# Cross attention in a Perceiver layer: another order at its first layer norm and in its last key block

## The chip, the core and the metric

The kernel runs on one core of a Trainium2 chip. Its time is the device time of one execution in microseconds (us). Five engines work side by side, each in the order of its own queue: TensorE (PE: matmuls into PSUM[...]), VectorE (DVE), ScalarE (ACT), GpSimd (POOL[...]) and SyncE (SP, which issues transfers). An instruction waits for the others by semaphores, and everything behind it in its queue waits with it.

## The reference

The layer is cross attention, self attention with relative positions and a gated attention block, each after a layer norm. The change touches the first:

```python
q = (query @ Wq + bq).reshape(Bq, Sq, H, DK)
k = (key @ Wk + bk).reshape(Bq, Sk, H, DK)
v = (value @ Wv + bv).reshape(Bq, Sk, H, DK)
scores = jnp.einsum('bqhd,bkhd->hbqk', q, k) / np.sqrt(DK)
attn = jax.nn.softmax(scores.reshape(H * Bq, Sq, Sk), axis=0).reshape(H, Bq, Sq, Sk)
out = jnp.einsum('hbqk,bkhd->bqhd', attn, v).reshape(Bq, Sq, H * DK)
return out @ Wo + bo
```

The query is layernorm(x), with 4 batches of 128 rows of 512; keys and values come from a context of 4 batches of 2048 rows. There are 16 heads of 32. The softmax runs over axis 0: for every pair of a query and a key, over the 64 combinations of head and batch. So a block of keys can be finished by itself: its maxima and sums run over heads and batches, not over other keys. All is float32.

## The kernel before

**Blocks.** The context is cut into 16 blocks n of 128 keys (NK = 16), and each block into 4 chunks c of 4 heads. For a chunk, `scores(n, c)` (line 277) writes 128 keys x 2048 numbers (4 heads x 4 batches x 128 queries) into four PSUM banks, two tiles of two banks. ScalarE copies them, half by half, to the tile `sg` (`scores_out`, line 298), and VectorE takes the running maximum `mx` of the same PSUM halves (`largest_of`, lines 305 and 307). After the fourth chunk, `largest_tail` (line 322) folds `mx` to one number per key and query. In the next block's turn each chunk is lowered by it (`shifted`, line 328, VectorE), put through the exponential (`exponentials_of`, line 337, ScalarE), and added up over heads and batches (`total`, lines 341 to 344, GpSimd; `total_tail` folds to `zs`). In the block after that, `inverse` (line 359) takes 1/z, `scaled` (line 328 again) multiplies each chunk by it, `attend` (line 372) multiplies with the values on TensorE into `pso`, and `accumulate` (line 385) adds `pso` to `acc`. So three blocks are in work at once: scores of n, exponentials of n-1, products of n-2.

**Projections.** `keys(n, c)` (line 220) and `values(n, b)` (line 227) are each four 128x512 matmuls into a bank of a pool of two (`bank`); ScalarE copies the bank out (lines 268 and 274), which frees it, and GpSimd adds the bias row of the values (line 275).

**The order** is written out by hand: each engine's queue holds its instructions in the order in which the Python code issues them. The banks of scores come from a pool of two tiles, so the next chunk's scores wait until both copies and both maxima of the last chunk have read theirs. Two engines don't read one PSUM tile at the same time here: the later in program order waits for the earlier. In blocks 0 and 1 a copy of one half and the maximum of the other stand in turn; from block 2 on both copies come first, then (`largest`, line 309) both maxima. `pso` has one bank.

**The start.** Keys of block 0; then `layernorm_T` (line 145) normalises x, and with `before` given it calls that after the normalisation, ahead of the four groups of transposes (`turned`, line 171, a pair of banks, ScalarE copies). Before is `values(0, 0)`. Then come four query projections (line 418), and in block 0's turn `values(0, c + 1)` ahead of each chunk's scores for c = 0, 1, 2; chunk 3 has `keys(1, 0)` there. `position_table` (line 111) is a generator that makes a table `pos` for the self attention in three steps: products on GpSimd; a matmul `pps`, a copy `prow` and two small transfers on SP's queue (through `pos_dram` into `posr`); a matmul `pflip` and the copy `pos`. The second step stands after scores (0,0), the third after those of (1,0).

**The end.** With l = 13, m = 14, n = 15: after the loop come the last attention product of block 13, block 15's `largest_tail`, its subtractions, exponentials and sums, the scalings of block 14, and the products. Half of chunk 2 and all of chunk 3 of block 15, and the sums that GpSimd made of the rest, are added up by TensorE: `sum_up` (line 508) multiplies by the identity into `ps_sum`. z is reduced from it (line 523). The output banks start from x1 (line 502) and collect `project_out` (line 529) as chunks of `acc` get ready; `layernorm_T(out_ps, ps_g, 1)` follows.

## Time and profile before

| | |
|---|---|
| median of 3 runs | 875.72 us (874.93 to 877.7) |
| the profiled execution | 875.97 us |
| its span in the profile | 874.1 us |
| TensorE busy | 830.6 us (95%) |
| VectorE, ScalarE, GpSimd busy | 628.2, 436.5, 430.6 us |
| first layer norm's transposes to the queries' first matmul | 22.8 to 26.3 us |
| last scores of block 15 | 599.7 to 600.8 us |
| last sum into `ps_sum` ends | 627.4 us |
| last output projection ends | 652.4 us |

In the profile's lines, "L227" is line 227 of the kernel before, the tiles follow as written <- read, then partitions x elements. A 128x512 float32 matmul shows as two records. The ends of matmuls are modelled, so records that follow each other overlap a little; from start to start a record of 512 columns takes 0.43 us at full clock. What stands in brackets is the idle time of the engine ahead of the group and what ended it.

### The profile page before, as it was taken

Reading aid. Unit: us, or ns where it says so; the run is one execution under the profiler, and the core shown is the slowest. Engines: PE = TensorE matmul, PEld = TensorE weight load, DVE = VectorE, ACT = ScalarE, POOL = GpSimd, SP = SyncE. Lnnn points to the kernel's source line nnn. Section 1 sums busy time; section 2 is a strip of 40 time slices with the busy share of each in tenths; the row PEclk is TensorE's granted clock in tenths of the full one; section 3 lists DMA queues with packets and bytes.
Section 4 is the critical chain, followed back from the end, with each engine's and each line's share of the span. In section 5 each row is a group of like instructions: output and inputs, shape, how many; then the busy total and the mean of one; then the engine's idle time right before and its main releaser. Section 6 shows DMA issues by size and latency. Waiting matters only on the chain. (4 is left out here: it accounts for less than half of the span.)

```text
span 874.1 us, 16373 instructions
## 1 busy us (share of the span) xinstructions
PE 830.6 (95%) x7061; PEld 447.9 (51%) x7061; DVE 628.2 (72%) x616; ACT 436.5 (50%) x721; POOL 430.6 (49%) x289
## 2 busy tenths in 40 slices
PE   9999999999999999999999999999898997779998
PEld 5454544554544545445445445544443466664564
DVE  2059788878888888888889888788861637556663
ACT  3357455564464554554554555644411736843671
POOL 1236666566656567575675665667500002512152
PEclk9999999999999999999999999999998998798999
DMA  8130010110101101010010101010100212001101
GB/s 300 50 124 2 1 49 1 49 49 1 50 1 49 49 2 49 1 49 13 37 49 1 49 1 49 1 36 15 49 28 21 96 50 98 1 2 51 49 1 49
DMA packets 10905, 35.53 MB, mean 41 GB/s; under 512 B 977, under 2 KB 1138, under 8 KB 8786
## 3 DMA queue, kind: packets, MB, share of 16 engines
q1 hardware_dynamic: 8402, 29.43, 9.7%
q10 hardware_dynamic: 1632, 3.15, 1.1%
q0 software_dynamic: 800, 1.93, 0.9%
q8 instruction: 55, 0.90, 0.4%
q14 instruction: 16, 0.13, 0.0%
HBM read 33.45 MB, written 1.05 MB: 39 GB/s over the span
## 5 line engine op out<-in xcount | busy, mean ns | idle before, releaser
L328 DVE TENSOR_TENSOR sg<-sg,stat 128x2048 f32<-128x2048 f32 x128 | 288.2, 2282 | 1.2
L337 ACT ACTIVATE sg<-sg 128x2048 f32<-128x2048 f32 x64 | 122.4, 1912 | 246.8 <-DVE sg L328 246.8
L227 PE MATMUL ps_v<-w_xattn_Wv,ct 128*128 128x512 f32 x512 | 231.5, 596 | 3.7 <-ACT v L274 3.7
L220 PE MATMUL ps_k<-ct,w_xattn_Wk 128*128 128x512 f32 x480 | 221.9, 605 | 0.8 <-ACT pos L142 0.8
L343 POOL TENSOR_TENSOR sm<-sm,sg 128x1024 f32<-128x1024 f32 x46 | 108.6, 2360 | 145.5 <-ACT sg L337 143.3
L307 DVE TENSOR_TENSOR mx<-mx,ps_s 128x1024 f32<-128x1024 f32 x96 | 117.2, 1221 | 78.1 <-ACT sg L298 65.9
L227 PEld LDWEIGHTS ps_v<-w_xattn_Wv,ct 128*128 128x128 f32 x512 | 95.8, 190 | 129.9 <-issue 113.5
L220 PEld LDWEIGHTS ps_k<-ct,w_xattn_Wk 128*128 128x128 f32 x480 | 86.2, 189 | 94.1 <-issue 86.1
L298 ACT COPY sg<-ps_s 128x1024 f32<-128x1024 f32 x128 | 124.2, 1020 | 7.2 <-DVE mx L305 3.5
L344 POOL TENSOR_TENSOR sm<-sm,sg 128x1024 f32<-128x1024 f32 x46 | 108.8, 2366 | 3.6
L275 POOL TENSOR_TENSOR v<-v,row_xattn_bv 128x512 f32<-128x512 f32 x64 | 81.6, 1276 | 40.0 <-ACT v L274 40.0
L734 POOL TENSOR_TENSOR lg<-lg,rs 128x512 f32<-128x512 f32 x16 | 16.3, 1041 | 120.9 <-issue 112.3
L285 PE MATMUL ps_s<-qT,kT 32*128 32x128 f32 x2048 | 75.7, 283 | 0.1
L372 PEld LDWEIGHTS pso<-sg,v 128*32 128x32 f32 x1920 | 48.8, 109 | 47.5 <-DVE mx L307 22.0
L285 PEld LDWEIGHTS ps_s<-qT,kT 32*128 32x128 f32 x2048 | 63.3, 186 | 18.0 <-issue 17.0
L372 PE MATMUL pso<-sg,v 128*32 128x128 f32 x1920 | 64.6, 276 | 3.7 <-DVE acc L385 2.1
L341 POOL TENSOR_TENSOR sm<-sg 128x1024 f32<-128x1024 f32 x16 | 37.9, 2366 | 45.3 <-ACT sg L337 45.2
L268 ACT ACTIVATE kT<-ps_k,bk 128x512 f32<-128x512 f32 x64 | 44.2, 694 | 10.4 <-PE ps_k L220 5.9
L274 ACT COPY v<-ps_v 128x512 f32<-128x512 f32 x64 | 36.4, 569 | 8.5 <-PE ps_v L227 8.4
L385 DVE TENSOR_TENSOR acc<-pso,acc 128x512 f32<-128x512 f32 x54 | 37.0, 684 | 3.9 <-PE pso L372 3.9
L305 DVE TENSOR_TENSOR mx<-sg,ps_s 128x1024 f32<-128x1024 f32 x16 | 19.5, 1220 | 27.3 <-ACT sg L298 27.3
L964 POOL TENSOR_TENSOR e<-e,rs 128x512 f32<-128x512 f32 x16 | 16.3, 1041 | 41.8 <-DVE rs L963 41.8
(208 smaller groups left out, 817.0 us busy)
## 6 DMA issues: line engine op xcount, KB each, us to landing
ct<-in_ctxT SPq DMA_DIRECT2D x15, 1024.0 KB, 4.9
ev_win<-in_tabv SPq DMA_DIRECT2D x1, 2048.0 KB, 7.1
w_xattn_Wk<-in_xattn_Wk ACTq DMA_DIRECT2D x4, 256.0 KB, 8.0
ct<-in_ctxT SPq DMA_DIRECT2D x4, 256.0 KB, 6.7
x<-in_x SPq DMA_DIRECT2D x4, 256.0 KB, 8.2
w_xattn_Wv<-in_xattn_Wv ACTq DMA_DIRECT2D x1, 1024.0 KB
w_xattn_Wq<-in_xattn_Wq SPq DMA_DIRECT2D x1, 1024.0 KB, 10.3
w_xattn_Wo<-in_xattn_Wo ACTq DMA_DIRECT2D x1, 1024.0 KB, 5.4
```

The lines of the kernel that those rows point to most:

```text
L220: nc.tensor.matmul(ps, lhsT=w[:, k, c * P : (c + 1) * P], rhs=src[:, k, :], start=(k == 0), stop=(k == C - 1))
L227: nc.tensor.matmul(ps, lhsT=src[:, k, b * T : (b + 1) * T], rhs=w[:, k, :], start=(k == 0), stop=(k == C - 1))
L268: nc.scalar.activation(kT[n, c], ps, AF.Identity, bias=bk[:, c : c + 1])
L275: nc.gpsimd.tensor_tensor(v[n, b], v[n, b], bv_row, ALU.add)
L285: nc.tensor.matmul(ps[i][:, cols], lhsT=kT[n, c][rows, cols], rhs=qT[rows, c, cols], start=True, stop=True)
L298: nc.scalar.copy(sg[n, c][:, k * HALF : (k + 1) * HALF], pss[n, c][k])
L307: nc.vector.tensor_tensor(mxs[n], mxs[n], pss[n, c][k], ALU.max)
L328: nc.vector.tensor_tensor(g, g, stat[:, row, :].unsqueeze(1).to_broadcast([P, NH * B, T]), op)
L337: nc.scalar.activation(sg[n, c], sg[n, c], AF.Exp, scale=SCALE)
L343: eng.tensor_tensor(t, t, g[:, 0:HALF], ALU.add)
L344: eng.tensor_tensor(t, t, g[:, HALF:], ALU.add)
L372: nc.tensor.matmul(ps[i * HD : (i + 1) * HD, b * T : (b + 1) * T], lhsT=v[n, b][:, h * HD : (h + 1) * HD], rhs=sg[n, c][:, f * T : (f + 1) ...
```

## The change

- **Layer norm 0.** `layernorm_T` takes a second callback, `after`, called behind the transposes. `values` is split into the matmuls (`values_into`) and copy plus bias (`values_out`). Values (0,0) go to the bank of `pso`, so the transposes have the pair of banks to themselves, and are copied out after the copies of the transposes. Values (0,1) follow there, ahead of the queries.
- **Block 0.** Values (0,2) and (0,3) stand at c = 0 and 1, where (0,1) and (0,2) stood; at c = 2 there is no projection. `pflip` and `pos` stand after scores (0,2).
- **The last chunk's maxima (15,3)** are taken in turn with the copies.
- **The end.** `scaled(13, 3)` and `accumulate(13, 2)` move behind the four subtractions of block 15, and `attend(13, 3)` behind the sums. Each projection `values(15, 1..3)` stands behind an exponential, from that of chunk 0 on. All of chunk 2 is summed by TensorE and none of it by GpSimd. `attend(14, 2)` moves behind `attend(15, 0)`. Values (15, 1..3) are held in the pool `tmp`, since block 13's are needed longer.

```diff
             before()
             for b in range(B):
                 turned(b)
+            after()
...
-        def values(n, b):
-            v[n, b] = vp.tile([P, D], F32, tag="v", name=f"v{n}_{b}")
-            ps = bank(f"v{n}_{b}")
+        def values(n, b, ps=None):
+            values_out(n, b, values_into(n, b, bank(f"v{n}_{b}") if ps is None else ps))
+
+        def values_into(n, b, ps):
             project(ps, wv, cts[n], b)
+            return ps
+
+        def values_out(n, b, ps):
+            if n == NK - 1 and b:
+                v[n, b] = tmp.tile([P, D], F32, tag="xn", name=f"v{n}_{b}")
+            else:
+                v[n, b] = vp.tile([P, D], F32, tag="v", name=f"v{n}_{b}")
             nc.scalar.copy(v[n, b], ps)
             nc.gpsimd.tensor_tensor(v[n, b], v[n, b], bv_row, ALU.add)
...
-            if n < 2:
+            if n < 2 or (n, c) == (NK - 1, C - 1):
                 for k in (1, 0):
                     scores_out(n, c, k)
                     largest_of(n, c, 1 - k)
...
-            if n >= 2:
+            if n >= 2 and (n, c) != (NK - 1, C - 1):
                 largest_of(n, c, 0)
                 largest_of(n, c, 1)
...
-        xT = layernorm_T([x1[:, b, :] for b in range(B)], ps_g, 0, before=lambda: values(0, 0))
+        ps = ps_o.tile([P, B * T], F32, tag="pso", name="ps_v0_0")
+        xT = layernorm_T(
+            [x1[:, b, :] for b in range(B)],
+            ps_g,
+            0,
+            before=lambda: values_into(0, 0, ps),
+            after=lambda: (values_out(0, 0, ps), values(0, 1)),
+        )
...
-                elif n == 0 and c + 1 < C:
-                    values(0, c + 1)
+                elif n == 0 and c + 2 < C:
+                    values(0, c + 2)
...
                 if n == 0 and c == C - 2:
+                    next(position)
...
                     exponentials_of(0, c)
                     total(0, c)
-                    if c == 0:
-                        next(position)
...
                         inverse(n - 2)
+                    if (n, c) == (NK - 1, C - 1):
+                        break
                     scaled(n - 2, c)
...
-        m, n = NK - 2, NK - 1
-        attend(*done)
+        l, m, n = NK - 3, NK - 2, NK - 1
         largest_tail(n)
-        values(n, 1)
-        shifted(n, 0)
-        exponentials_of(n, 0)
-        total(n, 0)
+        for c in range(C):
+            shifted(n, c)
+            exponentials_of(n, c)
+            if c < 2:
+                total(n, c)
+            if c + 1 < C:
+                values(n, c + 1)
+        scaled(l, C - 1)
         accumulate(*done)
-        values(n, 2)
-        shifted(n, 1)
-        exponentials_of(n, 1)
-        total(n, 1)
-        shifted(n, 2)
-        exponentials_of(n, 2)
-        values(n, 3)
-        half_total(n, 2)
-        shifted(n, 3)
-        exponentials_of(n, 3)
         inverse(m)
         scaled(m, 0)
-        scaled(m, 1)
...
-        sum_up(sg[n, 2][:, HALF:], True, False)
+        sum_up(sg[n, 2], True, False)
         sum_up(sg[n, 3], False, False)
         sum_up(sms[n], False, True)
-        attend(m, 0)
-        attend(m, 1, bank("m1"))
+        attend(l, C - 1)
+        attend(m, 0, bank("m0"))
+        scaled(m, 1)
         scaled(m, 2)
...
         inverse(n)
-        attend(m, 2, bank("m2"))
+        attend(m, 1, bank("m1"))
...
         scaled(n, 0)
+        accumulate(l, C - 1)
         attend(n, 0, pso[m, 0], True)
         accumulate(n, 0)
         scaled(n, 1)
+        attend(m, 2)
         project_out(0, range(B - 1))
```

More of the change, by code (lines that the diff above doesn't have):

```diff
@@ L143, in position_table, with layernorm_T @@
         yield
-    def layernorm_T(src, pool, n, before=None):
+    def layernorm_T(src, pool, n, before=None, after=None):
         st = small.tile([P, B, 6], F32, tag="st", name=f"st{n}")
```

## The prediction

> **What bounds the kernel now.** I read the page first, then the timeline of the two stretches that the diff touches (0 to 112 and 570 to 662 us), then busy time and clock in 2 us windows. Page, part 1:

> ```profile
> PE 830.6 (95%) x7061; PEld 447.9 (51%) x7061; DVE 628.2 (72%) x616; ACT 436.5 (50%) x721; POOL 430.6 (49%) x289
> ```

> TensorE is busy 95%, and 99.4 to 99.6 of each 100 us from 200 to 600: in the sixteen-block loop it is the bound. So what the change does ahead of block 2 is carried to the end at its full size; what it does at the other end counts by the chain there. Timeline of the start (start, length, engine, line; in brackets the idle time before and its releaser):

> ```profile
> 26.28 14.00 PE L220 MATMUL ps_q<-xT,w_xattn_Wq 128*128 128x512 f32 x32 [0.68 <-ACT xT L215]
> ...
> 50.00 3.70 PE L227 MATMUL ps_v<-w_xattn_Wv,ct 128*128 128x512 f32 x8
> 50.00 4.06 SPq L431 DMA_DIRECT2D ct<-in_ctxT  x2
> 50.10 2.55 DVE L307 TENSOR_TENSOR mx<-mx,ps_s 128x1024 f32<-128x1024 f32 x2 [2.95 <-PE ps_s L285]
> 50.16 1.01 ACT L298 COPY sg<-ps_s 128x1024 f32<-128x1024 f32 x1 [0.57 <-PE ps_s L285]
> ...
> 51.36 1.01 ACT L298 COPY sg<-ps_s 128x1024 f32<-128x1024 f32 x1 [0.18 <-DVE mx L307]
> ...
> 53.63 1.17 PE L285 MATMUL ps_s<-qT,kT 32*128 32x128 f32 x32
> ```

> Scores (0,1) start at 48.90; their four banks come free at 52.37 (second copy) and 52.65 (second maximum), 3.5 and 3.75 later. A `values` projection (50.00 to 53.6) lies over that, so scores (0,2) wait for nothing. Next, who releases the first attention product:

> ```profile
> 92.24 0.96 DVE L359 RECIPROCAL stat<-z 128x128 f32<-128x128 f32 x1 [5.16 <-POOL z L319]
> ```
> ```profile
> 95.58 1.08 PE L372 MATMUL pso<-sg,v 128*32 128x128 f32 x32 [0.21 <-DVE sg L328]
> ```

> TensorE meets a chain that hangs on block 0's last scores, not on TensorE's own pace: maxima, subtraction, copies, second exponential, six POOL additions and three folds from 74.90, reciprocal, scaling. At the end, TensorE and VectorE:

> ```profile
> 602.92 1.08 PE L372 MATMUL pso<-sg,v 128*32 128x128 f32 x32 [2.08 <-DVE acc L385]
> ...
> 625.41 1.99 PE L508 MATMUL ps_sum<-sm,ident 128*128 128x512 f32 x4 [1.10 <-POOL sm L352]
> ```
> ```profile
> 604.41 2.54 DVE L307 TENSOR_TENSOR mx<-mx,ps_s 128x1024 f32<-128x1024 f32 x2 [1.54 <-ACT sg L298]
> ```

> The last sums end at 627.40, and the reduction of z follows at 627.43; VectorE was done with (14,2) at 626.2. So 1.2 us is all that can be won there. Windows after the block loop (PE, PEld, DVE, ACT, POOL, then clock):

> ```profile
> 654.00:656.00 2.00, 1.31 (x8) 0.83 (x8) 1.06 (x4) 1.92 (x5) 0.00 (x0) 1.00 0.96 355
> 656.00:658.00 2.00, 1.58 (x8) 1.34 (x8) 1.56 (x3) 2.00 (x5) 0.00 (x0) 0.64 0.37 142
> 658.00:660.00 2.00, 1.17 (x3) 0.50 (x2) 0.82 (x2) 0.34 (x1) 0.00 (x0) 0.50 0.00 0
> ```

> The clock halves at 656.6 (0.64 is 28% at full, the rest at half) and is back at 663.4. Ahead of the drop TensorE was busy some 1.5 of 3.4 us.

> [...] the second copy (51.36) starts as the first maximum on its half ends.[...] 43% busy sufficed at 656.6, while 629.3 to 632.7 (windows of 3.4 counted back from there), with 58% busy, did not drop. My estimate of the limit is half a window.

> **Start, part by part.** (a) Layer norm: (0,0)'s copy goes behind the four xT copies, and its bank out of their pair. The second group of transposes no longer waits (0.24); groups three and four wait for a copy each, the fourth group at 24.65 (24.95 before). Values (0,1) start at 25.3 when the third copy is done; queries at 28.8, +2.5 against 26.28. The moved projection is 3.5, so 1.0 is gained. On POOL two bias additions stand ahead of five DMA issues, which so start near 30.7, not 24.9; the tabk0 product ends near 37.2, needed at 47.2: nothing. (b) Scores (0,0) at 46.1, (0,1) at 51.4 under the cover of values (0,3). (c) For (0,2) no projection is left. Scores (0,1) issue until 52.5; banks are free at 51.4 + 3.5 = 54.9 and 55.1. TensorE is idle 2.4 us, and (0,2) end issuing at 56.15 against 54.73: +1.4. (d) pflip now follows. It reads posr: prow 2.5 later, posr issued at 52.1, landing 4.5 later (DMA issues view) at 56.6; SP's ct load behind it is needed 16 us after it lands. Wait 0.45, pflip 0.33: keys (1,0), queued behind it, at 57.0 against 54.73, +2.25; scores (0,3) and VectorE's maxima wait for these. The pos copy leaves ScalarE's stretch between exponentials (0,0) and (0,1): -0.15. Old pflip and the 0.81 wait for pos at 70.60 lay beside the chain: their removal brings TensorE to the first attention product at +1.2 only, where it waits, since the chain from scores (0,3) through POOL to z is at 2.25 - 0.15. **Start: +2.1**; from +1.2 (POOL spans are rough; were its chain loose, TensorE alone counts) to +2.8 (posr a little later).

> (e) The clock. From 52.5 to 57.0 TensorE works 1.2 us on scores and 0.33 on pflip. With 2.4 to 2.85 idle, a 3.4 us window falls under half in about three of four phases. Half clock for one window then slows scores and keys (1,0), on the path, by 1.0 to 1.6. Over the phases I take 0.8; bounds 0 and 1.6.

> **End.** (f) Scores (15,3) issue until 600.77. First maximum 600.87 to 602.1; ScalarE passes exponential (14,3), a value copy and the half copy, 603.46; second maximum to 604.7 (606.95 before). Tail 1.97: subtraction (15,0) ends at 609.0, the others every 2.23 us until 615.7. Exponential (15,0) is done at 611.0. (g) TensorE: values (15,1) and (15,2) until 607.75. Values (15,3) needs the bank of (15,1), whose copy now stands behind exponential (15,0): 611.5. Behind it are queued x1, the sums and so z. That is 3.7 us idle in place of the old 2.08, 0.39, 0.30 and 1.10 with their drains. Then 8 records for values, 8 for x1, 20 for sums at 0.4286 (24 took 10.3): 15.4, done at 627.2 with the last drain of 0.27, against 627.40. POOL is ready at 619.5; leaving out the half total frees it, but four more sum records (1.7) are TensorE's. VectorE reaches (14,2) at 626.2 as before: scaling (13,3) and its accumulation are moved, not removed. (h) z is 0.15 earlier; attention (14,2), 1.0, fills the 0.81 wait after (15,0). Attention (15,1) starts at 636.2 both times (636.24 before). **End: -0.05**; from -0.8 to +0.4.

> (i) Its clock. A gap of 3.7 holds more than half a window at any phase. Half clock for a window, less what falls into the gap, costs 0.7 to 1.7 on values, x1 and sums, all ahead of z. I take 1.1; bounds 0 and 1.7. Other edits (tmp buffers for v, loop order, sg held longer: nine of ten buffers) cost nothing: no queue waits for them.

> **Sum.** 2.1 + 0.8 - 0.05 + 1.1 = +3.9: span 874.1 to 878.0. The profiled execution took 875.97, so 1.9 lies around the span; it is 0.25 above the median of 875.72. Median: 875.7 + 3.9 = 879.6.

> **Rivals.** (1) The clock holds in both gaps. For: a 2.08 gap at 600.8 left it at 1.00. Against: 656.6. Time 875.7 + 2.05 = 877.8, not slower by what can be told; it decides if a window needs to be nearly empty. (2) The bubble before (0,2) is hidden, since VectorE or POOL has slack that the trace doesn't show, and the layer norm's 1.0 is balanced by a small loss: 875 to 876. Against: the chain to z is continuous from 74.90. (3) Both ends pay: -1.0 at the layer norm and -1.2 at z, some 873.3, up to 0.8 less with the filled wait. It decides at a bubble under 1.0, that is banks free within 2.1 of the start of scores (0,1); the trace has 3.5, two turns of some 1.2 after 1.2 of scores.

> **How the numbers follow.** Forecast (a clock drop at one end at least, 878.4 to 882) 0.62; rival 1, 0.22; rival 2, 0.09; rival 3, 0.07. A measurement of this kernel tells 0.3%, 2.6 us, from no change. Slower 0.62, same 0.31, faster 0.07. Case range 878.4 to 882; the range of 875.5 to 882 takes in rival 1 and part of rival 2 and leaves some 0.18 outside.

> **What would show it.** Right: queries start near 28.8; a TensorE gap of 2.4 ahead of scores (0,2) released by ACT sg or DVE mx; pflip waits for posr; the first attention product near 97.7 or later; a gap of 3.7 ahead of values (15,3) released by ACT v; z reduced near 627.3 plus the start's shift; clock 0.5 after either gap. Wrong: no gap at (0,2), or z more than 1 us earlier than the shift allows.

## The result and the profile after

The changed kernel takes 881.56 us (median of 5, 878.66 to 884.54) against 875.72 us (874.93 to 877.7): ratio 1.0058, 95% interval 1.0031 to 1.0084. It is slower, by less than 1%. Timed again with 21 executions, it took 881.24 against 877.20, ratio 1.0034 (1.0025 to 1.0044). The forecast was 879.6, which is +3.9; the two measurements are +5.8 and +4.0 by their medians, +5.1 and +3.0 by their ratios.

The page's first part of the changed kernel:

```profile
PE 833.7 (95%) x7065; PEld 449.5 (51%) x7065; DVE 628.0 (71%) x616; ACT 435.6 (49%) x721; POOL 427.6 (49%) x288
```

TensorE is busy 3.1 us more. Four more sum records are 1.7 of it; the rest is put down to records at half clock. To see where the added time went, both profiled executions (875.97 and 882.15 us) are cut at the same instructions:

| stretch (us) | before | after | difference |
|---|---|---|---|
| span's start to first matmul of values (0,0) | 19.34 | 20.38 | +1.04 |
| from there to the first attention product ("start") | 76.24 | 80.36 | +4.12 |
| to scores (15,3) | 504.09 | 503.96 | -0.13 |
| to the reduction of z ("end") | 27.76 | 29.32 | +1.56 |
| to the last group of output projections ("tail") | 20.35 | 20.35 | 0.00 |
| to the span's end | 226.32 | 226.03 | -0.29 |
| span | 874.1 | 880.4 | +6.3 |

The first row is no effect of the change: its work begins after it, and over the nine profiled executions of the experiments it lies anywhere from 19.41 to 20.52. The two ends hold the rest. TensorE's timeline at the start (columns as in the prediction):

```profile
26.42 3.70 PE L228 MATMUL ps_v<-w_xattn_Wv,ct 128*128 128x512 f32 x8 [0.19 <-ACT xT L216]
29.95 13.90 PE L221 MATMUL ps_q<-xT,w_xattn_Wq 128*128 128x512 f32 x32
...
52.47 1.17 PE L294 MATMUL ps_s<-qT,kT 32*128 32x128 f32 x32
55.99 1.44 PE L294 MATMUL ps_s<-qT,kT 32*128 32x128 f32 x32 [2.35 <-ACT sg L307]
58.29 0.79 PE L141 MATMUL ps_pflip<-flip,posr 128*128 128x128 f32 x2 [0.86 <-DMA posr<-pos_dram]
58.88 4.93 PE L221 MATMUL ps_k<-ct,w_xattn_Wk 128*128 128x512 f32 x8
...
100.74 1.08 PE L381 MATMUL pso<-sg,v 128*32 128x128 f32 x32 [0.88 <-DVE sg L337]
```

Less the 1.04, values (0,1) start at 25.4, the queries at 28.9, scores (0,1) at 51.4; then come 2.35 idle for the banks, released by ScalarE's copy (54.93 to 55.94; it had itself waited 0.18 for VectorE's maximum of the same half), and 0.86 for `posr`. Keys (1,0), behind pflip in the queue, start at 58.88 and take 4.93 where eight records take 3.6 at full clock. VectorE shows what lies ahead of the attention product: the same wait for z from GpSimd as before, only later.

```profile
97.40 0.96 DVE L368 RECIPROCAL stat<-z 128x128 f32<-128x128 f32 x1 [5.25 <-POOL z L328]
```

The end, TensorE, then VectorE, then ScalarE:

```profile
605.80 7.13 PE L228 MATMUL ps_v<-w_xattn_Wv,ct 128*128 128x512 f32 x16
616.57 5.40 PE L228 MATMUL ps_v<-w_xattn_Wv,ct 128*128 128x512 f32 x8 [3.63 <-ACT v L283]
621.80 3.60 PE L511 MATMUL ps_out<-x,ident 128*128 128x512 f32 x8
625.24 7.03 PE L517 MATMUL ps_sum<-sg,ident 128*128 128x512 f32 x16
632.10 1.88 PE L517 MATMUL ps_sum<-sm,ident 128*128 128x512 f32 x4
```
```profile
605.91 1.22 DVE L316 TENSOR_TENSOR mx<-mx,ps_s 128x1024 f32<-128x1024 f32 x1 [0.82 <-PE ps_s L294]
608.51 1.22 DVE L316 TENSOR_TENSOR mx<-mx,ps_s 128x1024 f32<-128x1024 f32 x1 [1.38 <-ACT sg L307]
...
634.02 0.69 DVE L533 TENSOR_REDUCE z<-ps_sum 128x128 f32<-128x512 f32 x1 [3.01 <-PE ps_sum L517]
```
```profile
614.13 1.91 ACT L346 ACTIVATE sg<-sg 128x2048 f32<-128x2048 f32 x1 [4.74 <-DVE sg L337]
615.95 0.57 ACT L283 COPY v<-ps_v 128x512 f32<-128x512 f32 x1
```

The maxima do end earlier, and the copy that frees the bank for values (15,3) does stand behind exponential (15,0): TensorE idles 3.63. VectorE has 3.01 to spare before z, so TensorE sets z. Its eight value records took 5.40 where 3.70 is usual: these 1.7 us are the clock's.

Busy time by engine in windows of 3.41 us, the length of the shortest period of half clock in this profile (PE, PEld, DVE, ACT, POOL, then granted clock, DMA share and GB/s); the edges are counted from where half clock begins:

```profile
54.70:58.12 3.42, 1.44 (x32) 1.25 (x32) 2.24 (x3) 1.70 (x3) 3.42 (x3) 1.00 0.67 215
58.12:61.53 3.41, 3.24 (x6) 1.69 (x7) 1.61 (x2) 1.55 (x3) 1.29 (x2) 0.50 0.90 377
...
614.51:617.92 3.41, 1.35 (x3) 0.68 (x4) 3.41 (x2) 3.41 (x3) 2.92 (x3) 1.00 0.00 0
617.92:621.33 3.41, 3.41 (x5) 1.35 (x4) 3.41 (x3) 2.69 (x3) 3.41 (x3) 0.50 0.00 0
```

After a window with TensorE busy for 1.44 (42%) and after one with 1.35 (40%), the next whole window runs at 0.50.

### The profile page after: what moved, and what is told of

It reads as the page before. It is cut to its first block, busy times and chain, and to the rows that moved or that the text cites. A ratio compares the mean times of both kernels' runs of the same rounds, so it can differ in the third digit from the quotient of the medians.

```text
span 880.4 us, 16375 instructions
## 1 busy us (share of the span) xinstructions
PE 833.7 (95%) x7065; PEld 449.5 (51%) x7065; DVE 628.0 (71%) x616; ACT 435.6 (49%) x721; POOL 427.6 (49%) x288
## 3 DMA queue, kind: packets, MB, share of 16 engines
HBM read 33.45 MB, written 1.05 MB: 39 GB/s over the span
## 4 chain that ended last, share of the span: by engine, by line
DVE 35%; PE 32%; ACT 21%; issue 11%; POOL 1%; DMA 1%; ACTq 0%; DVEq 0%; POOLq 0%
DVE sg L337 14%; DVE mx L316 12%; ACT sg L307 10%; ACT sg L346 4%; ACT v L283 3%; DVE stat L331 3%; PE s_k L221 3%; PE s_v L228 3%; PE ps_v L228 3%; PE ps_k L221 2%; DVE mx L314 2%; PE s_q L221 2%; PE s_y L1063 2%; PE ps_k L409 2%; PE s_q L228 2%
## 5 line engine op out<-in xcount | busy, mean ns | idle before, releaser
L352 POOL TENSOR_TENSOR sm<-sm,sg 128x1024 f32<-128x1024 f32 x46 | 108.5, 2359 | 145.5 <-ACT sg L346 143.4
L307 ACT COPY sg<-ps_s 128x1024 f32<-128x1024 f32 x128 | 124.1, 1020 | 8.1 <-DVE mx L314 3.5
```

Of the source, the lines that this page charges most:

```text
L307: nc.scalar.copy(sg[n, c][:, k * HALF : (k + 1) * HALF], pss[n, c][k])
L352: eng.tensor_tensor(t, t, g[:, 0:HALF], ALU.add)
```

## The experiments

Theory: the start is slower by a wait that the moved projection uncovers, with half clock on top; the end has no more than the clock's part. Rivals: the end alone makes the loss; the wait costs nothing and only the clock does; or the position table's step is what delays the keys. All kernels compute the whole reference; one has two extra matmuls, named below. Times are given as ratios to the kernel before on the same chip, with 95% intervals. The stretches come from one profiled execution each. The last column is the granted clock of a whole execution, as the mean over all executions of the kernel (their number in brackets), then the same for the kernel before on that chip. One more window of half clock lowers it by 0.002 (half of 3.41 us in some 876):

| kernel | start | end | tail | ratio | mean clock; before |
|---|---|---|---|---|---|
| before | 76.24 | 27.76 | 20.35 | 1 | |
| changed, first profile | 80.36 | 29.32 | 20.35 | 1.0058 (1.0031 to 1.0084) | 0.9786 (5) |
| e1, start undone | 76.22 | 30.38 | 20.34 | 0.9993 (0.9978 to 1.0008) | 0.9817 (14); 0.9798 (43) |
| e2, end undone | 79.63 | 27.74 | 22.04 | 1.0037 (1.0024 to 1.0050) | 0.9782 (6); 0.9798 (43) |
| e3, cover back | 76.27 | 29.34 | 20.34 | 0.9995 (0.9983 to 1.0007) | 0.9811 (14); 0.9798 (43) |
| e4, x1 first | 79.41 | 26.24 | 20.33 | 1.0009 (1.0000 to 1.0018) | 0.9817 (21); 0.9798 (43) |
| e0, changed again | 79.86 | 27.62 | 20.35 | 1.0034 (1.0025 to 1.0044) | 0.9791 (21); 0.9800 (34) |
| e5, filler | 78.16 | 29.18 | 20.35 | 1.0023 (1.0012 to 1.0035) | 0.9811 (14); 0.9800 (34) |
| e6, flip back | 79.46 | 29.32 | 20.35 | 1.0030 (1.0018 to 1.0043) | 0.9804 (16); 0.9803 (19) |
| e8, both mended | 75.62 | 26.23 | 21.99 | 0.9949 (0.9936 to 0.9961) | 0.9832 (5); 0.9800 (34) |
| e7, GpSimd scales | 75.63 | 24.88 | 20.02 | 0.9932 (0.9919 to 0.9945) | 0.9836 (5); 0.9800 (34) |

The diffs are against the changed kernel, unless said otherwise.

### e1: the start undone

```diff
-            before=lambda: values_into(0, 0, ps),
-            after=lambda: (values_out(0, 0, ps), values(0, 1)),
-        )
+        xT = layernorm_T([x1[:, b, :] for b in range(B)], ps_g, 0, before=lambda: values(0, 0), after=lambda: None)
...
-                elif n == 0 and c + 2 < C:
-                    values(0, c + 2)
+                elif n == 0 and c + 1 < C:
+                    values(0, c + 1)
...
                 if n == 0 and c == C - 2:
-                    next(position)
...
+                    if c == 0:
+                        next(position)
```

> The change's end with the start of the kernel before. Theory (lost cover in block 0 and half clock after it, +4.1 at the start; copies behind exponentials and half clock, +1.6 at the end): 875.7 + 1.6 = 877.3 us, first attention product where it was (about 95.6), gap of 3.6 us ahead of values (15,3) and half clock after it still there. Rival (the end alone costs the time, and the start's lateness is a later first matmul): 880 to 881 us.

The start is 76.22, as before. The end in the profiled execution is 30.38, with two windows of half clock, more than in the changed kernel. Yet by its times (median 876.13 of 14, where 877.3 was expected) the kernel equals the one before. The profiled execution took 879.47, the slowest of the 14: it overstates the end. The mean clock of all 14 is 0.9817, above the 0.9798 of the kernel before: over whole executions, the new end with the old start brings no more half clock than the old kernel had.

### e2: the end undone

The kernel before with only the start's edits: the callbacks of the layer norm, `c + 2`, and pflip after scores (0,2). The end is line for line the old one.

> The change's start with the end of the kernel before. Theory: 875.7 + 4.1 = 879.8 us; the 2.4 us gap ahead of scores (0,2) stays, the first attention product about 4 us late against the first matmul, and the last sums end about 28 us after the last scores, as before. Rival (the end alone costs): 875.7 to 876.5 us.

Start +3.39, and 0.37% by time, 3.2 us of 877.6 (2.0 by the medians of 6 and 43 executions). So the start makes the significant part of the loss. In this profiled execution half clock also fell on the tail, which is the old code here. TensorE's timeline of e2:

```profile
637.75 4.54 PE L541 MATMUL ps_out<-w_xattn_Wo,acc 128*128 128x512 f32 x6 [0.81 <-DVE acc L391]
```

Six records took 4.54 where 2.8 is usual: half clock strikes in the old end too, in some executions. Another window of it, from 607.2 on, slowed the last projections of block 15 (24 records in 11.30 us, 10.57 before), and yet the end is 27.74: the old end's waits of 0.39, 0.30 and 1.10 ahead of the sums shrank to one of 0.73 and took it up. The execution of before which the prediction was made from had half clock in neither place.

### e3: the cover back

One condition: values (0,2) and (0,3) stand ahead of scores (0,1) and (0,2) again, as in the kernel before, with the rest of the change kept. Ahead of scores (0,0) nothing stands now.

```diff
-                elif n == 0 and c + 2 < C:
-                    values(0, c + 2)
+                elif n == 0 and 0 < c < C - 1:
+                    values(0, c + 1)
```

> The changed kernel with values (0,2) ahead of scores (0,1) and values (0,3) ahead of scores (0,2), and nothing ahead of scores (0,0). Theory (the cover of scores (0,2) is what is lost): no 2.4 us gap ahead of scores (0,2), no half clock there; scores (0,0) wait 0.9 us for the last query copy, which the layer norm's filling pays; start at about -0.2 to +0.2, time 877.3 us as with the start undone. Rival (the layer norm's new order itself is late, or pflip's wait is what costs): 880 to 881.5 us.

TensorE's timeline of e3:

```profile
49.70 3.70 PE L228 MATMUL ps_v<-w_xattn_Wv,ct 128*128 128x512 f32 x8
53.33 1.17 PE L294 MATMUL ps_s<-qT,kT 32*128 32x128 f32 x32
```

The projection covers the turns of copies and maxima, scores (0,2) wait for nothing, the clock holds, and the start is 76.27. The wait of 0.9 that was expected ahead of scores (0,0) isn't there: they follow the queries at 43.05. With the new end in place the ratio is 0.9995, so this one condition undoes the whole of the measured loss.

### e4: x1 first

The four identity matmuls that put x1 into the output banks wait for nothing that block 15 makes. They move into the gap.

```diff
+            if c == 2:
+                out_ps, _ = banks("out")
+                for b in range(B):
+                    nc.tensor.matmul(out_ps[b], lhsT=ident, rhs=x1[:, b, :], start=True, stop=False)
             if c + 1 < C:
                 values(n, c + 1)
...
-        out_ps, _ = banks("out")
-        for b in range(B):
-            nc.tensor.matmul(out_ps[b], lhsT=ident, rhs=x1[:, b, :], start=True, stop=False)
```

> The changed kernel with the eight matmuls of x1 moved ahead of values (15,3), where TensorE waits 3.6 us. Theory (gap and half clock are on the path to z): gap under 0.4 us, clock at 1.00 there, sums end before VectorE is through with scaling (14,2), z about 2.6 us earlier against the last scores; 881.6 - 2.6 = 879.0 us. Rival (z isn't on the path, or VectorE's tail sets the end): less than 0.5 us gained, 881 us or more.

TensorE's timeline of e4:

```profile
611.16 3.60 PE L505 MATMUL ps_out<-x,ident 128*128 128x512 f32 x8
614.96 3.70 PE L228 MATMUL ps_v<-w_xattn_Wv,ct 128*128 128x512 f32 x8 [0.20 <-ACT v L283]
```

and VectorE's:

```profile
622.72 6.68 DVE L337 TENSOR_TENSOR sg<-sg,stat 128x2048 f32<-128x2048 f32 x3
629.32 0.68 DVE L534 TENSOR_REDUCE z<-ps_sum 128x128 f32<-128x512 f32 x1
```

The gap of 3.63 became 0.20, and the end is 26.24, 1.5 under that of before. z now follows VectorE's third scaling without a wait: VectorE sets it. By time the kernel gains about 0.25% on the changed one (878.14 on one chip, 881.24 on another, each against its own before).

### e0: the changed kernel again

> The changed kernel once more, beside the others on one chip. Theory: some 5 us above the kernel before; from the first values to the first attention product 79.4 to 80.5 us (76.2 before), from the last scores to the reduction of z 29 to 30.5 us (27.8 before), from there to the last output projections 20.35 us as before. Rival (the two chips differ more than the two kernels): less than 2.6 us above.

The same gap, without the clock's part, first in the timeline of TensorE and then by windows:

```profile
615.56 3.70 PE L228 MATMUL ps_v<-w_xattn_Wv,ct 128*128 128x512 f32 x8 [3.63 <-ACT v L283]
```
```profile
610.28:613.69 3.41, 1.65 (x4) 0.38 (x2) 3.38 (x3) 0.57 (x1) 3.33 (x4) 1.00 0.00 0
613.69:617.10 3.41, 1.54 (x4) 0.83 (x5) 3.41 (x2) 3.41 (x3) 2.97 (x3) 1.00 0.00 0
617.10:620.51 3.41, 3.41 (x10) 1.50 (x9) 3.41 (x3) 3.41 (x5) 3.41 (x3) 1.00 0.04 7
```

The edge fell almost at the middle of the gap. Both windows keep 48% and 45% of work, and the clock stayed at 1.00. The end is then 27.62, 0.14 under that of before, where 29 to 30.5 was expected; the time, +4.0 by medians, is under the 5 expected too. The start, 79.86, is as expected: half clock came again there (43% busy in the window ahead of it). This profiled execution is the fastest of the 21 (878.15), as e1's was the slowest of its own.

### e5: a filler in the start's gap

Two more 128x512 matmuls stand ahead of scores (0,2); nobody reads what they write.

```diff
+                if (n, c) == (0, C - 2):
+                    ps = ps_o.tile([P, B * T], F32, tag="pso", name="filler")
+                    for k in range(2):
+                        nc.tensor.matmul(ps, lhsT=cts[0][:, k, 0:P], rhs=wv[:, k, :], start=True, stop=True)
                 scores(n, c)
```

> The changed kernel with two matmuls of 128x512 more, whose result nobody reads, in the 2.4 us gap ahead of scores (0,2). Theory (the lost cover is 2.3 to 2.7 us by itself, half clock another 0.9 to 1.4): clock stays at 1.00, keys (1,0) take 3.7 us again, first values to first attention product 78.5 to 79.1 us, about 1 us below the changed kernel. Rival (the wait alone, or posr, sets the lateness, whatever the clock): as the changed kernel, or up to 1.7 us above it by the added work.

TensorE's timeline of e5:

```profile
53.13 1.98 PE L471 MATMUL filler<-w_xattn_Wv,ct 128*128 128x512 f32 x4
55.55 1.44 PE L294 MATMUL ps_s<-qT,kT 32*128 32x128 f32 x32 [0.44 <-ACT sg L307]
57.19 0.49 PE L141 MATMUL ps_pflip<-flip,posr 128*128 128x128 f32 x2 [0.20 <-DMA posr<-pos_dram]
57.52 3.60 PE L221 MATMUL ps_k<-ct,w_xattn_Wk 128*128 128x512 f32 x8
```

Scores (0,2) start no earlier, but keys (1,0) take 3.60: full clock. What remains, +1.92, is the wait's own price (2.3 to 2.7 was expected); the half clock is the other 1.7 of e0's +3.62. It isn't this one execution only: the mean clock of all 14 is 0.9811, and 0.9791 for e0 on the same chip, which is one window of half clock less in the mean. By time it is 0.11% under e0, with intervals that overlap: the stretches separate the two, the times hardly do.

### e6: pflip back in block 1

```diff
                 if n == 0 and c == C - 2:
-                    next(position)
...
+                    if c == 0:
+                        next(position)
```

> The changed kernel with one edit: the third step of the position table (the matmul pflip and the copy pos) stands in block 1 again, after scores (1,0), as before. The gap ahead of scores (0,2) stays. Theory of step (d): keys (1,0) wait no more for posr (0 to 0.86 in the executions so far) nor for pflip (0.33), so the stretch from the first matmul of values (0,0) to the first attention product shrinks from 79.9 to 80.4 to some 79.0, with the half clock in it, or to 77.6 if the clock holds; the gap ahead of scores (0,2) reads 2.35 again. Rival: keys (1,0) or scores (0,3) wait for something else at the same time (the banks of scores (0,2), the copies of keys), and the stretch stays within 0.3 of 79.9. Time by the theory 0.5 to 1.0 us under the changed kernel, by the rival none; both within what the rounds can tell, so the stretch decides.

TensorE's timeline of e6:

```profile
55.38 1.44 PE L294 MATMUL ps_s<-qT,kT 32*128 32x128 f32 x32 [2.35 <-ACT sg L307]
56.76 5.36 PE L221 MATMUL ps_k<-ct,w_xattn_Wk 128*128 128x512 f32 x8
```

The start is 79.46, between theory (79.0) and rival (79.6 at least), so neither number was met. Keys (1,0) follow the scores at once, so nothing else waits there and the rival's mechanism is absent. The window of half clock (56.72 to 60.13) falls wholly on work and costs its full 1.7; the theory's number had 1.4 for it. That leaves +1.5 for the wait. By time it can't be told from e0.

### e8 and e7: both ends mended, and GpSimd scales

e8 joins e3, e4 and e6. e7 adds this to it, with 1/z of block 14 copied to a tile of its own (`inv`) by ScalarE:

```diff
+        def scaled_pool(n, c):
+            g = sg[n, c].rearrange("p (f q) -> p f q", q=T)
+            nc.gpsimd.tensor_tensor(g, g, inv.unsqueeze(1).to_broadcast([P, NH * B, T]), ALU.mult)
...
         scaled(m, 1)
-        scaled(m, 2)
+        scaled_pool(m, 2)
+        scaled_pool(m, 3)
...
-        scaled(m, 3)
```

> The changed kernel with values (0,2) and (0,3) at chunks 1 and 2, pflip back in block 1, and x1 ahead of values (15,3). Theory: start -0.75 us against before (scores (0,2) covered, pflip off the chain), end -1.5 us; 2.2 us below the kernel before. Rival (VectorE's and ScalarE's chains set both ends anyway): within 0.5 us of the kernel before.

> As e8, and the scalings of (14,2) and (14,3) go to GpSimd, which is idle then, from a copy of 1/z in SBUF. Theory (z waits for VectorE's scaling once TensorE's gap is filled): z 1.4 us earlier than in e8, tail up to 0.6 us shorter; 3.5 to 4 us below the kernel before. Rival (GpSimd's two scalings, 4.7 us each, come late, or slow VectorE beside them): a TensorE wait ahead of attention (14,2) of 1 us or more, no gain over e8.

e8: start -0.62, end -1.53, and a window of half clock in the tail (+1.6); 873.58 us against 877.20, ratio 0.9949. So the change's ideas are worth something at both ends once the gaps are closed: 0.6 is the layer norm's 1.0 less small losses (scores (0,0) start 23.40 after the first values, 24.30 before; 0.62 of this 0.90 is left at scores (0,2)), and it shows once pflip, with its wait of 0.54 for `posr`, is off the path, which e3 (76.27) had not done. e7's VectorE and GpSimd timelines:

```profile
624.86 0.69 DVE L543 TENSOR_REDUCE z<-ps_sum 128x128 f32<-128x512 f32 x1 [0.44 <-PE ps_sum L526]
```
```profile
622.29 9.08 POOL L517 TENSOR_TENSOR sg<-sg,inv 128x2048 f32<-128x2048 f32 x2
```

With one scaling taken from ahead of z, z waits 0.44 for TensorE's sums again, and the end is 24.88, 2.9 under that of before. e7 takes 872.17 us (871.26 to 873.01) against 877.20: ratio 0.9932, faster than both kernels. No wait ahead of attention (14,2) shows, so the rival of late scalings is absent.

Both kernels gained more than was expected (2.2 and 3.5 to 4), and more than start, end and tail add up to: 0.5 for e8 in its profile, 3.8 for e7, where the medians fell by 3.6 and 5.0. Their mean clock is higher than that of before by one and a half to two windows of half clock, over five executions each. Why they meet fewer was not tested, so the gain beyond the stretches is not shown to be the edits' own.

## Why the prediction came out as it did

The direction, the places and the order of causes were right. The clock was mis-sized at both ends: too low at the start, and at the end counted for the new kernel alone.

**(a), (b), layer norm.** Predicted +2.5 for the queries against the first values; measured +2.63 (9.57 against 6.94). Of the 1.0 that was to come back later, e8 shows 0.90 at scores (0,0) and 0.62 at the attention product; in e3 pflip and its wait for `posr` take it.

**(c), (d), the bubble and pflip.** The idle time of 2.4 measured 2.35, in all five executions that have it without a filler. The path's share was +1.4 for the bubble, 0.33 for pflip, -0.15 for the moved copy and 0.45 for `posr`. Here `posr` was the loose term: its wait was 0.86, 0.27, 0, 0 and 0.20 (changed, e0, e2, e4, e5). With each one's own wait the sum gives 2.44, 1.85, 1.58, 1.58 and 1.78; without the clock's part (1.62 in the first, whose window held 0.17 of idle time; 1.7 in the next three; none in e5) the starts show 2.50, 1.92, 1.69, 1.47 and 1.92. Within 0.15, the working holds. It stands on the chain from scores (0,3) to z: the filler filled TensorE and won nothing but the clock.

**(e), the clock at the start.** This step failed in size. It was given 0.8 as a mean over phases, of 1.0 to 1.6 when it happens. It happened in all five executions with the bubble open, and cost 1.6 to 1.7: the window falls on scores (0,2) and keys (1,0), all work on the path. "Three of four phases" isn't refuted by five, but three quarters of the 1.7 measured would have been an estimate nearer 1.3. That half clock lasts one window was the author's estimate too; in the changed kernel it lasted 3.413 us there (58.14 to 61.55).

**(f) to (h), the end.** Without the clock, e0's end is -0.14 where z was to be 0.15 earlier, the gap is 3.63 for 3.7, and the tail is unchanged. The working was right to a tenth.

**(i), the clock at the end.** The limit of half a window was wrong: e0 has the gap at full clock, though both its windows are under half busy (48% and 45%), as the step said of any phase. Half clock came in five of six executions with that gap (the changed kernel's first, e1, e3, e5, e6), and cost 1.6 to 1.7 with one window and 2.8 with two (e1), against the 1.1 taken and the bound of 1.7. Still, the times show none of it: e1 and e3 equal the kernel before. The step put the old kernel's own half clock at nothing, since the one trace had none ahead of 656. But the old kernel pays as well (e2, +1.7 in the tail), and the difference of the two is what counts. Over all executions the mean clock of e1 and e3 (0.9817, 0.9811) is no lower than that of before (0.9798). Where the windows fall is seen only in the profiled executions.

**The sum.** Predicted +2.9 for the start and +1.05 for the end. In the first profile it was +4.12 and +1.56, with +1.04 of chance ahead of both. By times, the start is +0.37% (e2) and the end nothing that can be told from zero (e1, e3). The median of 21 executions, +4.0, meets the +3.9; by the ratio it is +3.0 (2.2 to 3.9), and the forecast stands at the upper edge. That the sum came so near is partly luck: the start cost more than forecast in every profile that has the gap and half clock (3.17 to 4.12 for 2.9), and the end cost less by the times.

**The rivals.** (1), the clock holds: fallen at the start, five of five; it came true once in six at the end. (2), the bubble is hidden: fallen, e5 has +1.92 without half clock there. (3), both ends pay: fallen for the change as made. The gains it spoke of exist (-0.6 and -1.5 in e8), but at the end only when TensorE's queue has work for the gap, and the limit was then VectorE, as the prediction had it (1.2 to be won, 1.5 measured). Its time was mis-added: 875.7 less 2.2 is 873.5, not 873.3.

## What to carry to other kernels

Before a projection is moved to fill one gap, look at what it covers where it stands: here 3.5 us of matmuls lay over 3.5 us of bank turns, and the move won 1.0 and uncovered 2.35. In this kernel TensorE's gaps of 2.35 and 3.63 us cost a part of their length (+1.92 in e5; 1.4 from e0 to e4) and, when half clock followed, up to 1.7 us for each window of it where what came next was on the path; work that waits for nothing (x1 by the identity) is the first candidate to stand in it. Judge a loss of this size by many executions and by stretches, and count the old kernel's half clock too: in single profiles it came and went with the phase.

## What the runs showed that was not expected

```profile
607.98:611.39 3.41, 1.05 (x3) 0.19 (x1) 3.41 (x2) 1.15 (x1) 3.33 (x4) 1.00 0.00 0
611.39:614.80 3.41, 2.12 (x3) 1.09 (x4) 3.41 (x3) 3.41 (x4) 2.97 (x4) 0.50 0.00 0
```

**The untouched rest moves by 2 us.** What follows the tail is the same code in all eleven kernels. In the profiles it takes 224.2 to 224.7 us in five (e0, e4, e5, e7, e8), with about seven windows of half clock in it (worked out from the mean clock of each, less the windows at its start, end and tail), and 225.9 to 226.3 us in the other six, with about nine, and ten in before. So the time of one profiled execution can't judge a change worth 3 us, and the difference of the spans, +6.3 in the first profiles, is only +2.1 from before to e0 (874.1 and 876.2 us).

**GpSimd beside VectorE.** In e7 a scaling of 128x2048 took GpSimd 4.54 and VectorE 2.29, while the two overlapped. VectorE took 2.29 in e8 as well, where GpSimd was idle beside it. No run has GpSimd's scaling alone; its additions of half that size (128x1024) took 2.36 to 2.38 in e7, so 4.54 is under twice that. No slowing of VectorE by GpSimd is seen in this, and whether GpSimd was slowed is not shown.
